# Routing beside RWKV6 with one operand in PSUM, counts sorted by expert, tables of experts built by segments, and the last piece's sends a page sooner

## The chip, the core and the metric

The kernel runs on one core of one Trainium2 chip. The metric is the device time of one execution in microseconds (us); less is better. All data are 32-bit floats.

## What is computed

The input x has 4 sequences of 1024 tokens with 256 channels. Four blocks are added to it, each behind a layer norm:

```python
x = x + retention(layernorm(x))   # 16 heads, decay mask, group norm, gate
x = x + moe(layernorm(x))         # 8 experts, the best 2 of each token
x = x + rwkv6(layernorm(x))       # a recurrence over 1024 tokens, 16 heads of 16x16 states
x = x + moe(layernorm(x))         # the same experts
```

In the MoE the two highest of eight logits of a token choose its experts; their softmax weights, normed to a sum of one, weigh the two results. An expert is `silu(gate) * up` of 256 to 2 x 256 channels, and a product back to 256.

## The kernel before, in words

Retention, MoE, RWKV6 and MoE again follow one another, with some overlap at the borders. A tile has 128 partitions.

**MoE.** Tokens are sorted by expert through DRAM. The 4096 tokens are 32 tiles; they come in three pieces (`Piece`, called m or next_a for the first 16 tiles, mid and end for 8 each). For each piece `logits` makes the router's products on PE, `biased` (L524) adds the bias on DVE, and `routing` (L534 to L730), a generator that `route` advances by one part a call, works on DVE: a token's two best experts (`m_top`, `m_eq`, `m_where`, `m_hot`, `m_rest`, L553 to L563), their softmax (`m_dif`, `m_ex`, `m_den`, `m_tag`, L573 to L584), the tokens before it with the same expert by two matmuls with triangles of ones (`m_rank`, L589 and L590), counts and prefix sums (`m_cnt`, `m_run`, L593 and L595), pages of each expert (`m_more`, `m_pages`, `m_first`), and each token's two rows in the sorted table (`m_off`, `m_eq`, `m_atf`, `m_at`, L675 to L694). The last part makes the table of experts (`m_reach`, `m_of`, `m_ofi`, L702 to L730): which expert's weights each of 71 pages needs. `send` then writes a token tile: ACT makes `m_row` (L495, and L735 for the tags), and POOL issues two indirect DMAs to `xg_all` (L737).

`tiles` then goes over the 71 pages of 128 rows. In iteration j PE transposes page j+1 (`m_xtp`, L781; ACT copies it to `m_xt`, L783), multiplies page j (`m_hp`, L788), transposes page j-1 (`m_atp`, L818) and multiplies page j-2 (`m_op`, L825). ACT makes `m_sg` (L792), DVE `m_a` (L794) and `m_aT` (L820) and, for each group of four pages, `m_share` and `m_to` (L803 to L813). ACT weighs the result (`m_y`, L830), and POOL sends it back (L831, `y_all`). Pages are loaded from `xg_all` in groups of four by SP (L770). Pages 0 to 24 hold tokens of the first piece only, so their work starts while mid and end are still routed and sent; page 25 and later ones wait for all sends. A dictionary names what else comes in which iteration (`add(j, f)`): routing, sends, and the finish of the stage before.

**RWKV6.** Eight blocks of 512 tokens, each of eight steps (step 8j + n) of two halves. In a half DVE multiplies (`w_vb`, L1094) and makes two scans (`w_s`, L1096), POOL multiplies by r (`w_s`, L1104), and PE sums (`w_yp`, L1127). PE, ACT, DVE and POOL prepare the next block beside that (`w_pp`, L1008; `w_dp`, L964; `w_xf`, L974 to L978) and finish the last one (`w_sq`, L1183; `w_rstd`, L1167; `w_cen`, L1181 and L1182). Piece next_a is routed in steps 44 to 46 and sent from step 47 on; mid's routing begins in steps 61 to 63.

**What sets the order.** PE's and ACT's instructions run in the order in which the program writes them, all through; DVE's and POOL's too from the first MoE on, and SP's in RWKV. In retention the scheduler orders DVE. Small results lie in SBUF. PSUM is given out in banks of 128x512; products take the next of a ring of three (`psum`, tag "mm"), which waits for the bank's former readers. A routing's m_rank takes one of those.

The calls that place routing, sends and tables among the pages are these:

```python
for n in range(PARTS - 3):
    add(n // 2, mid.route)
for i in range(mid.nt):
    add(3 + i, mid.send, i)
...
for n in range(PARTS):
    add(9 + n // 2, end.route)
for i in range(end.nt):
    add(13 + i, end.send, i)
```

Of the kernel before, what the change touches and what calls it, by code (L numbers as in the profile page):

```python
# [53 lines left out]
E = 8  # L54
# [54 lines left out]
def hybrid_kernel(  # L109
# [360 lines left out]
    class Piece:  # L470


        def __init__(self, moe, start, blocks, prev=None):
            self.moe, self.start, self.prev = moe, start, prev
            self.nt = blocks * NT
# [59 lines left out]
        def routing(self):  # L535
            sm, logit, nt = self.sm, self.logit, self.nt

# [8 lines left out]

            tops, hots, wheres = [], [], []
            cur = logit  # L550
            for n in range(2):
                top = sm([HT], f"m_top{n}")
                nc.vector.tensor_reduce(top, cur, AX.X, ALU.max)  # L553
                eq = sm([HT, E], f"m_eq{n}")
                nc.vector.tensor_tensor(eq, cur, wide(top), ALU.is_equal)
                nc.vector.tensor_mul(eq, eq, per(key))
                where = sm([HT], f"m_where{n}")
                nc.vector.tensor_reduce(where, eq, AX.X, ALU.max)
                hot = sm([HT, E], f"m_hot{n}")
                nc.vector.tensor_tensor(hot, eq, wide(where), ALU.is_equal)  # L560
                if n == 0:
                    cur = sm([HT, E], "m_rest")
                    nc.vector.scalar_tensor_tensor(cur, hot, NEG, logit, ALU.mult, ALU.add)  # L563
                tops.append(top)
                wheres.append(where)
                hots.append(hot)
                if n == 0:
                    yield
# [3 lines left out]
            dif = sm([HT], "m_dif")  # L572
            nc.vector.tensor_sub(dif, tops[1], tops[0])  # L573
            ex = sm([HT], "m_ex")
            nc.scalar.activation(ex, dif, AF.Exp)
            yield
            den = sm([HT], "m_den")
            nc.vector.tensor_scalar_add(den, ex, 1.0)
            tag = self.tag = sm([HT, 4], "m_tag", bufs=2)
            nc.vector.reciprocal(tag[:, :, 0], den)  # L580
            nc.vector.scalar_tensor_tensor(
                tag[:, :, 1], ex, -1.0, tag[:, :, 0], ALU.add, ALU.mult)
            nc.vector.tensor_copy(tag[:, :, 2], dest[:, self.start * NT : self.start * NT + nt])
            nc.vector.tensor_scalar(  # L584
                tag[:, :, 3], wheres[0], -1.0, float(E), ALU.mult, ALU.add)
            both = both.rearrange("p i e -> p (i e)")

            rp = psum([P, 2, nt * E], "m_rank")
            mm(rp[:, 0, :], lhsT=before, rhs=both, start=True, stop=True)  # L589
            mm(rp[:, 1, :], lhsT=every, rhs=both, start=True, stop=True)  # L590
            yield
            cnt = sm([E, HT], "m_cnt")
            nc.vector.tensor_copy(cnt, rp[:, 1, :].rearrange("p (i e) -> p e i", e=E))  # L593
            run = sm([E, HT], "m_run")
            nc.vector.tensor_tensor_scan(  # L595
                run.rearrange("p e i -> p (e i)"), chains[nt],
                cnt.rearrange("p e i -> p (e i)"), 0.0, ALU.mult, ALU.add,
            )

            def pages(name, total, n, op=ALU.is_gt, first=0):  # L600
                more = (ph if n == HT else px).tile([P, E, n], F32, name="m_more", tag=f"m_more{n}")
                nc.vector.tensor_tensor(
                    more, each(total, n), steps[:, first : first + n].unsqueeze(1).to_broadcast(
                        [P, E, n]), op)
                t = sm([E], name)
                nc.vector.tensor_reduce(t, more, AX.X, ALU.add)
                return t
# [17 lines left out]
            prev, last = self.prev, run[:, :, nt - 1]  # L625
            cap = sm([E], "m_cap")
            self.segments = []
            if prev is None:

                self.total = last  # L630
                full = pages("m_whole", last, HT, ALU.is_ge, 1)
                self.pages = pages("m_pages0", last, HT)
                part = sm([E], "m_part")
                nc.vector.tensor_sub(part, self.pages, full)
                f, behind = firsts("m_first0", full, 0.0)
                self.segments.append(f)
                nc.vector.tensor_scalar_mul(cap, full, float(P))
                low = sm([E], "m_low")
                nc.vector.tensor_scalar_mul(low, f, float(P))
                f, self.used = firsts("m_first1", part, behind)  # L640
                self.segments.append(f)
                self.counts = sm([E], "m_counts0")
                nc.vector.tensor_copy(self.counts, last)
                high = begins("m_high0", f, cap)
                shifted = low
            else:
                k = prev.order + 1
                self.counts = sm([E], f"m_counts{k}")
                nc.vector.tensor_add(self.counts, prev.counts, last)
                self.pages = pages(f"m_pages{k}", self.counts, TT)  # L650
                part = sm([E], "m_part")
# [4 lines left out]
                low = prev.open  # L656
                high = begins(f"m_high{k}", f, cap)
                shifted = sm([E], "m_low")
                nc.vector.tensor_add(shifted, low, prev.counts)
            self.order = 0 if prev is None else prev.order + 1  # L660
            rise = sm([E], "m_rise")
            nc.vector.tensor_sub(rise, high, low)

            if prev is None:
                self.open = high
            else:
                self.open = sm([E], f"m_open{self.order}")
                nc.vector.scalar_tensor_tensor(
                    self.open, part, 0.0, rise, ALU.is_gt, ALU.mult)
                nc.vector.tensor_add(self.open, self.open, low)  # L670
            nc.vector.tensor_add(cap, cap, low)
            yield

            off = sm([E, HT], "m_off")
            nc.vector.tensor_sub(off, run, cnt)  # L675
            nc.vector.tensor_add(off, off, each(shifted))
            slot = sm([HT, E], "m_eq0")
            nc.vector.tensor_add(
                slot, rp[:, 0, :].rearrange("p (i e) -> p i e", e=E),
                off.rearrange("p e i -> p i e"),  # L680
            )
            new = sm([HT, E], "m_eq1")
            nc.vector.tensor_tensor(new, slot, per(cap), ALU.is_ge)
            nc.vector.tensor_mul(new, new, per(rise))
            nc.vector.tensor_add(slot, slot, new)
            yield
            self.at = []
            for n in range(2):
                t = sm([HT, E], "m_rest")
                nc.vector.tensor_mul(t, hots[n], slot)  # L690
                f = sm([HT], f"m_atf{n}")
                nc.vector.tensor_reduce(f, t, AX.X, ALU.add)
                a = sm([HT], f"m_at{n}", I32, bufs=2)
                nc.vector.tensor_copy(a, f)  # L694
                self.at.append(a)
            yield
# [3 lines left out]
            if prev is None:  # L700
                lo, n, parts = 0, FULL, self.segments[:1]
            else:  # L702
                lo, n, parts = FULL, NSL - FULL, self.segments
            if prev is not None and self.start + nt // NT < NBLK:
                return
            at = number[:, lo : lo + n]
            where = ph if lo == 0 else px
            of = where.tile([P, n], F32, name="m_of", tag=f"m_of{lo}")
            for k, f in enumerate(parts):
                reach = where.tile(  # L710
                    [P, n, E - 1], F32, name="m_reach", tag=f"m_reach{lo}")
                nc.vector.tensor_tensor(
                    reach, at.unsqueeze(2).to_broadcast([P, n, E - 1]),
                    f[:, 1:E].unsqueeze(1).to_broadcast([P, n, E - 1]), ALU.is_ge)
                if k == 0:
                    nc.vector.tensor_reduce(of, reach, AX.X, ALU.add)
                    continue
# [5 lines left out]
                if k == 2:  # L723
                    yield
            ofi = where.tile([P, n], I32, name="m_ofi", tag=f"m_ofi{lo}")
            nc.vector.tensor_copy(ofi, of)
            for j in range(n):
                moe.ofi[lo + j] = ofi[0:1, j : j + 1]
            moe.ofs.append((lo, of))
# [707 lines left out]
    PARTS = 8  # L1437
    m, mid = moes[0].pieces[:2]
    for i in range(CHUNKS):
# [12 lines left out]
        if i in (24, 25):  # L1452
            for _ in range(PARTS // 2):
                m.route()
        if i >= 26:
# [7 lines left out]
    for _ in range(3):  # L1463
# [18 lines left out]
    def pieces_sent(mid, end, logits):  # L1482

        for n in range(PARTS - 3):
            add(n // 2, mid.route)
        for i in range(mid.nt):
            add(3 + i, mid.send, i)
# [3 lines left out]
        for n in range(PARTS):  # L1491
            add(9 + n // 2, end.route)
        for i in range(end.nt):
            add(13 + i, end.send, i)
# [17 lines left out]
    add(7, end.block, 1)  # L1512
    pieces_sent(mid, end, ((0, 7), (1, 9)))
# [36 lines left out]
    for n in range(PARTS):  # L1550
        add(44 + n // 3, next_a.route)
    for n in range(3):
        add(61 + n, mid.route)
# [27 lines left out]
    add(6, end.block, 1)  # L1581
    pieces_sent(mid, end, ((1, 8),))
# [124 lines left out]
```

## Time and profile before

| what | value |
|---|---|
| median of 3 runs (lowest, highest) | 1609.24 us (1603.85, 1613.45) |
| profiled execution: its time, its span | 1602.58 us, 1600.8 us |
| mean granted clock of PE | 0.898 |
| busy: PE, DVE, POOL, ACT | 1358.1, 1017.4, 925.8, 604.6 us |
| RWKV6, from the first to the last w_s | about 675 to 1297 us |
| pages 0 to 24 of the first MoE | about 355 to 482 us |
| pages 0 to 24 of the second MoE | about 1299 to 1427 us |

A row of a timeline gives start, duration in us, engine, line, operation, result and operands with their shapes, a count, and in brackets the idle time of the engine before it and what released it. In the chain of waits, a row is a piece of the chain that ended last; "issue" is time in which an engine waited for nothing that the profile shows. PE, DVE, ACT and POOL are TensorE, VectorE, ScalarE and GpSimd; SP issues most DMAs.

### The profile page before, as it was taken

The page shows a single profiled execution, that of the slowest core. Times are in us where ns is not written, and L with a number is a line of the kernel's source. Part 1 is how long each engine was busy: PE and PEld are TensorE (multiplying, and loading weights), DVE is VectorE, ACT ScalarE, POOL GpSimd, SP SyncE. Part 2 cuts the span into 40 slices and gives each one's busy share as a digit, 9 for nine tenths or more (in the row PEclk, how much of TensorE's full clock was granted, in tenths as well). Part 3 has the DMA queues.
Part 4 walks back from the last instruction along what each step waited for, and adds up shares of the span by engine and source line. Part 5 has one row for each costly group of instructions (what it writes and reads, how often), then busy time and mean ns, then how long its engine had stood idle before and what let it go on. Part 6 is the DMA issues. An engine that isn't in the chain of part 4 may idle for free.

```text
span 1600.8 us, 21021 instructions
## 1 busy us (share of the span) xinstructions
PE 1358.1 (85%) x6652; PEld 715.6 (45%) x6652; DVE 1017.4 (64%) x2004; ACT 604.6 (38%) x1436; POOL 925.8 (58%) x881
## 2 busy tenths in 40 slices
PE   5999999878889988987879798887697587889993
PEld 3667666545545544422223233332232234456562
DVE  6566557424433443387988898999989962523444
ACT  2343434433433334443343434442344224333331
POOL 4233322744463326399999898986599844453331
PEclk9999999968899999998989798997789778899997
DMA  8991111231333431266655444533346832232545
GB/s 294 331 321 54 54 45 49 72 119 56 125 102 102 133 111 55 63 150 149 166 140 154 119 133 112 150 105 106 98 126 162 258 110 77 90 108 93 187 130 181
DMA packets 117548, 207.70 MB, mean 130 GB/s; under 512 B 12193, under 2 KB 80001, under 8 KB 117441
## 3 DMA queue, kind: packets, MB, share of 16 engines
q1 hardware_dynamic: 95904, 160.20, 34.7%
q0 software_dynamic: 17184, 39.86, 8.0%
q10 hardware_dynamic: 4352, 6.29, 1.3%
q8 instruction: 57, 0.93, 0.2%
q14 instruction: 51, 0.41, 0.1%
HBM read 139.18 MB, written 67.14 MB: 129 GB/s over the span
## 4 chain that ended last, share of the span: by engine, by line
PE 53%; DVE 18%; POOL 13%; ACT 6%; issue 5%; DMA 4%; SPq 0%; DVEq 0%; POOLq 0%; ACTq 0%
PE m_hp L788 13%; PE m_op L825 6%; DVE w_s L1096 5%; POOL w_s L1104 5%; PE w_pp L1008 4%; PE a_qkp L291 3%; DVE w_vb L1094 2%; PE a_yp L350 2%; PE w_dp L964 2%; PE m_lp L520 2%; PE w_yp L1127 2%; PE a_sp L330 2%; POOL xg_all L737 2%; PE a_gp L273 2%; PE m_xtp L781 2%
## 5 line engine op out<-in xcount | busy, mean ns | idle before, releaser
L1104 POOL TENSOR_TENSOR w_s<-w_s,w_rT 128x1024 f32<-128x1024 f32 x128 | 304.2, 2417 | 33.9 <-DVE w_s L1096 30.3
L831 POOL DMA_INDIRECT y_all<-m_y,m_to x142 | 137.6, 969 | 300.6 <-ACT m_xt L783 171.2
L788 PE MATMUL m_hp<-w1a,m_xt 128*128 x568 | 287.7, 632 | 15.2 <-ACT m_xt L783 11.8
L794 DVE TENSOR_TENSOR m_a<-m_hp,m_sg 128x256 f32<-128x256 f32 x142 | 60.1, 423 | 292.6 <-ACT m_sg L792 292.5
L1094 DVE TENSOR_TENSOR w_vb<-w_vb,w_wk 128x1024 f32<-128x1024 f32 x128 | 153.3, 1198 | 30.5 <-ACT w_wk L1037 26.6
L1096 DVE TENSOR_TENSOR_SCAN w_s<-w_wk,w_carry,w_vb 128x512 f32<-128x512 f32 x128 | 160.9, 1275 | 9.3 <-PE w_yp L1127 1.2
L1096 DVE TENSOR_TENSOR_SCAN w_s<-w_wk,w_vb 128x512 f32<-128x512 f32 x128 | 152.8, 1215 | 13.3 <-ACT w_carry L1114 5.9
L825 PE MATMUL m_op<-w2a,m_aT 128*128 x568 | 152.7, 393 | 6.2 <-DVE m_aT L820 4.5
L737 POOL DMA_INDIRECT xg_all<-m_row,m_at x128 | 125.8, 982 | 43.5 <-issue 29.2
L788 PEld LDWEIGHTS m_hp<-w1a,m_xt 128*128 128x128 f32 x568 | 103.9, 204 | 91.8 <-issue 78.4
L1127 PE MATMUL w_yp<-w_s,core_c 128*32 128x512 f32 x512 | 101.2, 690 | 45.3 <-POOL w_s L1104 34.8
L792 ACT ACTIVATE m_sg<-m_hp 128x256 f32<-128x256 f32 x142 | 54.5, 384 | 165.3 <-PE m_hp L788 165.3
L303 POOL TENSOR_TENSOR a_t<-a_t,a_t 128x512 f32<-128x512 f32 x32 | 41.1, 1285 | 125.9 <-DVE a_t L302 94.1
L830 ACT ACTIVATE m_y<-m_op,m_share 128x256 f32<-128x256 f32 x142 | 67.3, 474 | 119.6 <-PE m_op L825 119.6
L977 POOL TENSOR_TENSOR w_xf<-w_xf,w_sx 128x512 f32<-128x512 f32 x72 | 94.1, 1307 | 24.3 <-ACT w_xf L976 23.6
L825 PEld LDWEIGHTS m_op<-w2a,m_aT 128*128 128x128 f32 x568 | 99.9, 196 | 18.0 <-ACT m_sg L792 3.6
L978 POOL TENSOR_TENSOR w_xf<-w_xf,w_xT 128x512 f32<-128x512 f32 x80 | 87.2, 1093 | 5.6
L333 DVE TENSOR_TENSOR a_pt<-a_sp,ret_c 128x2048 f32<-128x2048 f32 x32 | 73.2, 2286 | 17.6 <-PE a_sp L330 17.5
L818 PEld LDWEIGHTS m_atp<-cst,m_a 128*128 128x128 f32 x284 | 40.6, 146 | 90.3 <-issue 65.9
L781 PE MATMUL m_xtp<-cst,m_xg 128*128 128x128 f32 x284 | 58.6, 290 | 15.2 <-DMA m_xg<-xg_all 15.2
L783 ACT COPY m_xt<-m_xtp 128x256 f32<-128x256 f32 x142 | 51.9, 366 | 42.8 <-PE m_xtp L781 42.6
L291 PE MATMUL a_qkp<-wqkv,a_xT 128*128 128x512 f32 x128 | 65.9, 641 | 0.0
(251 smaller groups left out, 2461.0 us busy)
## 6 DMA issues: line engine op xcount, KB each, us to landing
w_vb<-v_all SPq DMA_DIRECT2D x125, 512.0 KB
xg_all<-zero SPq DMA_DIRECT2D x34, 520.0 KB
m_xg<-xg_all SPq DMA_DIRECT2D x34, 520.0 KB
tab<-in_rope SPq DMA_DIRECT2D x32, 512.0 KB
m_back<-y_all SPq DMA_DIRECT2D x48, 256.0 KB
v_all<-w_vT SPq DMA_DIRECT2D x64, 128.0 KB
res<-in_x SPq DMA_DIRECT2D x8, 512.0 KB
w1a<-in_w SPq DMA_DIRECT2D x8, 512.0 KB
```

Source lines behind the costliest of these rows:

```text
L291: mm(qkp, lhsT=xc[:, c, cols], rhs=wqkv[:, c, 0 : 2 * C], start=(c == 0), stop=(c == KC - 1))
L737: nc.gpsimd.indirect_dma_start(out=self.moe.sends[2 * (self.start * NT + i) + n][:, :], out_offset=bass.IndirectOffsetOnAxis(ap=self.at[n] ...
L781: nc.tensor.transpose(tp[:, c, :], self.xg[g][:, i, c * P : (c + 1) * P], ident)
L788: mm(hp, lhsT=self.xt[j][:, c, :], rhs=w1a[:, bass.ds(self.ev[j], 1), c, :].rearrange("p o n -> p (o n)"), start=(c == 0), stop=(c == KC - 1))
L825: mm(op, lhsT=self.aT[j][:, c, :], rhs=w2a[:, bass.ds(self.ev[j], 1), c, :].rearrange("p o n -> p (o n)"), start=(c == 0), stop=(c == KC - 1))
L831: nc.gpsimd.indirect_dma_start(out=self.scatters[j][:, :], out_offset=bass.IndirectOffsetOnAxis(ap=self.to[g][:, i : i + 1], axis=0), in_= ...
L977: nc.gpsimd.tensor_mul(xf, xf, sx)
L978: nc.gpsimd.tensor_add(xf, xf, d["now"][:, c, :])
L1094: nc.vector.tensor_mul(vb, vb, wk[:, 1:2, :].to_broadcast([P, 2, BLK]))
L1096: nc.vector.tensor_tensor_scan(s[:, q, 1 : BLK + 1], wk[:, 0, :], vb[:, q, :], 0.0 if j % NB == 0 else st[j - 1]["carry"][:, n, 2 * h + q ...
L1104: nc.gpsimd.tensor_mul(s[:, :, 0:BLK], s[:, :, 0:BLK], d["r"][:, g, :].unsqueeze(1).to_broadcast([P, 2, BLK]),)
L1127: mm(d["yp", g][32 * q : 32 * q + 32, :], lhsT=w["sel"][:, i, :], rhs=d["s", n, q // 2][:, q % 2, 0:BLK], start=False, stop=(i == 3), skip ...
```

## The change

- In the piece next_a (`apart`), routing's temporaries lie in two PSUM banks: the choice of experts in a bank m_choice, the later ones in the bank of m_rank. So each two-input DVE operation of it has at most one operand in SBUF. ACT copies hot0 and the counts (128x128 each) to SBUF.
- In all six pieces the two matmuls take m_both sorted by expert, so ranks and counts come out sorted, the copy m_cnt goes, and slots are computed in that order. den, reciprocal and tag follow the scan.
- The table of experts is a method, `table(k)`, for one segment a call. Routing has 6 parts (4 in next_a) in place of 8.
- The calls move. Retention: the first piece is routed in chunks 24 and 25 (three parts each) with its table in 25; mid gets 2 parts there (3 before). First MoE: mid's parts in iterations 1, 1, 2, 3 (0, 0, 1, 1, 2 before). Second MoE: 1, 2, 3 (the same five before). Both: mid's sends in iterations 4 to 11 (3 to 10), end's parts in 9, 9, 10, 11, 11, 11 (two each in 9 to 12), end's sends in 12 to 19 (13 to 20), tables in 6, 7, 14 and 18 (all with end's last part in 12). RWKV6: next_a's parts in steps 44, 44, 45, 46 (three, three and two in 44 to 46), its table in step 62 (46).

The diff, cut to its core:

```diff
+            self.apart = prev is None and moe.layer == 1
...
+        def bank(self, name):
+            self.room = psum([P, 512], name)
+            self.col = 0
+
+        def tmp(self, shape, name):
+            if not self.apart:
+                return self.sm(shape, name)
+            n = int(np.prod(shape))
+            t = self.room[:, self.col : self.col + n]
+            self.col += n
+            return t if len(shape) == 1 else t.rearrange("p (a b) -> p a b", b=shape[1])
...
+            if self.apart:
+                self.bank("m_choice")
...
+            eq = tmp([HT, E], "m_eq")
             for n in range(2):
-                top = sm([HT], f"m_top{n}")
+                top = (tmp, sm)[n]([HT], f"m_top{n}")
...
-                hot = sm([HT, E], f"m_hot{n}")
+                hot = (tmp, sm)[n]([HT, E], f"m_hot{n}")
...
             nc.scalar.activation(ex, dif, AF.Exp)
+            if self.apart:
+                hot = sm([HT, E], "m_hot0")
+                nc.scalar.copy(hot, hots[0])
+                hots[0] = hot
             yield
...
-            both = both.rearrange("p i e -> p (i e)")
-            rp = psum([P, 2, nt * E], "m_rank")
+            both = both.rearrange("p i e -> p e i")
+            rp = psum([P, 512], "m_rank")
+            self.room, self.col = rp, 2 * nt * E
...
-            cnt = sm([E, HT], "m_cnt")
-            nc.vector.tensor_copy(cnt, rp[:, 1, :].rearrange("p (i e) -> p e i", e=E))
-            run = sm([E, HT], "m_run")
+            if self.apart:
+                each_cnt = sm([E, HT], "m_cnt")
+                nc.scalar.copy(each_cnt, cnt)
+            else:
+                each_cnt = cnt
+            run = tmp([E, HT], "m_run")
...
+        def table(self, k):
...
-        for n in range(PARTS - 3):
-            add(n // 2, mid.route)
         for i in range(mid.nt):
-            add(3 + i, mid.send, i)
+            add(4 + i, mid.send, i)
...
         for n in range(PARTS):
-            add(9 + n // 2, end.route)
+            add((9, 9, 10, 11, 11, 11)[n], end.route)
         for i in range(end.nt):
-            add(13 + i, end.send, i)
+            add(12 + i, end.send, i)
+        add(6, mid.table, 0)
+        add(7, mid.table, 1)
+        add(14, mid.table, 2)
+        add(18, end.table, 3)
...
+    for n, j in enumerate((1, 1, 2, 3)):
+        add(j, mid.route)
...
-    for n in range(PARTS):
-        add(44 + n // 3, next_a.route)
-    for n in range(3):
-        add(61 + n, mid.route)
+    for n in (44, 44, 45, 46):
+        add(n, next_a.route)
+    add(62, next_a.table, 0)
+    for n in (61, 62, 63):
+        add(n, mid.route)
...
+    for n, j in enumerate((1, 2, 3)):
+        add(j, mid.route)
```

## The prediction

> **What bounds the kernel now.** I read the table of 40 slices first (no engine fills the span), then the page's chain:
>
> ```profile
> PE 53%; DVE 18%; POOL 13%; ACT 6%; issue 5%; DMA 4%; SPq 0%; DVEq 0%; POOLq 0%; ACTq 0%
> ```
>
> The bound changes by stage, so I took timelines where the change edits. First the DVE, then POOL, in RWKV's steps 44 to 47:
>
> ```profile
> 1094.28 1.46 DVE L555 TENSOR_TENSOR m_eq<-m_logit,m_top 128x128 f32<-128x128 f32 x1
> 1095.77 1.24 DVE L556 TENSOR_TENSOR m_eq<-m_eq,cst 128x128 f32<-128x128 f32 x1
> 1097.05 0.29 DVE L558 TENSOR_REDUCE m_where<-m_eq 128x16 f32<-128x128 f32 x1
> 1097.37 1.99 DVE L560 TENSOR_TENSOR m_hot<-m_eq,m_where 128x128 f32<-128x128 f32 x1
> ...
> 1116.06 2.56 DVE L595 TENSOR_TENSOR_SCAN m_run<-cst,m_cnt 128x128 f32<-128x128 f32 x1
> ...
> 1123.03 0.29 DVE L685 TENSOR_TENSOR m_eq<-m_eq,m_eq 128x128 f32<-128x128 f32 x1
> ...
> 1325.92 0.30 DVE L1164 SCALAR_TENSOR_TENSOR w_varp<-w_varp,q_y 128x128 f32<-128x128 f32 x1
> ```
>
> ```profile
> 1096.83 2.38 POOL L1104 TENSOR_TENSOR w_s<-w_s,w_rT 128x1024 f32<-128x1024 f32 x1
> ...
> 1128.76 2.35 POOL L1104 TENSOR_TENSOR w_s<-w_s,w_rT 128x1024 f32<-128x1024 f32 x1 [10.43 <-DVE w_s L1096]
> ```
>
> A 128x128 operation with two SBUF inputs takes 0.29 us when POOL is idle (L685) and up to 1.99 beside it; m_hot ends at 1099.36, where POOL's w_s ends (1099.21). The reduce with one input, 0.29, isn't held. POOL then idles 10.43 us for the DVE: routing is on the path there.
>
> In the first MoE, PE, then POOL:
>
> ```profile
> 367.84 2.63 PE L788 MATMUL m_hp<-w1a,m_xt 128*128 x4 [3.14 <-DVE m_eq L678]
> ...
> 376.59 3.78 PE L788 MATMUL m_hp<-w1a,m_xt 128*128 x4 [3.80 <-ACT m_xt L783]
> ...
> 445.02 0.69 PE L818 MATMUL m_atp<-cst,m_a 128*128 128x128 f32 x2 [3.61 <-DVE m_a L794]
> 446.59 2.04 PE L825 MATMUL m_op<-w2a,m_aT 128*128 x4 [0.88 <-DVE m_aT L820]
> ...
> 481.94 0.66 PE L781 MATMUL m_xtp<-cst,m_xg 128*128 128x128 f32 x2 [4.92 <-DMA m_xg<-xg_all]
> ```
>
> ```profile
> 442.80 1.16 POOL L737 DMA_INDIRECT xg_all<-m_row,m_at  x1 [0.30 <-DVE m_ofs L721]
> 449.42 0.96 POOL L831 DMA_INDIRECT y_all<-m_y,m_to  x1 [5.46 <-ACT m_y L830]
> ...
> 475.19 0.96 POOL L737 DMA_INDIRECT xg_all<-m_row,m_at  x1 [0.30 <-issue]
> ```
>
> DVE's 6.4 us of tables (438.15 to 444.64) stop PE, which starves POOL for 5.46 us; from there POOL issues back to back, and page 25's load waits for its last send. The second MoE repeats this (PE waits 3.60, 0.87 and 4.92 us); the chain shows the end:
>
> ```profile
> 1420.20 2.46 DMA xg_all<-m_row,m_at
> 1422.84 4.00 DMA m_xg<-xg_all
> 1426.97 0.53 PE m_xtp L781 x2
> ```
>
> **RWKV (next_a's routing).** Step 44: from 1093.99 to 1105.68, seven held operations cost 1.46 + 1.24 + 1.99 + 1.24 + 0.81 + 1.23 + 0.81 = 8.78 us; at 0.29 each (2.03) they save 6.7. Gone too is the wait for m_ex (0.28). den, reciprocal and tag (0.6) move to step 46: nothing. m_run goes from 2.56 to about 0.42 (an unheld 128x128 scan in retention): 2.1. The copy m_cnt: 0.27. The table (0.31 + 0.34 + 1.92 = 2.57, step 46) moves to step 62. Sum 11.9; added: the first PSUM write waits for ACT's reading of that bank's former tile, 0.7 by the ACT row near 1094.7. Queued behind it on DVE are step 45's scans, which POOL waits for. Net 11.2.
>
> [...] But L1164 on PSUM takes 0.30, L685 on SBUF 0.29, and only strided reads more (L678 0.37). [...] Copies of hot0 and counts go to ACT, 38% busy, at an estimated 0.2 to 0.4 each (m_xt's copy of 256 is 0.37); the routing's second half comes two steps (7 us) later and hides them; uncovered, 0.7.
>
> Does POOL take over? Its queue ends at 1104.08, then only w_s of 2.36 a scan pair, and its 10.43 us idle is larger than what is taken out. And PE: m_choice and m_rank hold two of the ring of three banks, the latter to the last routing operation; w_pp (L1008) now waits for that. Before, it had 12 us of lead. Its chain runs about 7 us, its product is needed some 10.6 us after step 47 starts: estimated slack 3.7; for w_dp 3. Cost 0 to 3, taken 0. At step 62 the table pays again: 0.6 for its two first operations, 0.2 to 1.9 for the cast, of which some falls into a POOL operation the next routing row would wait out anyway: 1.2. RWKV: -10 (range -5 to -11.5). Sends and weight loads follow the steps in program order.
>
> **First MoE, opening.** The retention tail's a_mean to a_shift now stand ahead of mid's scan on DVE. a_shift came at 371.85 behind 4.7 us of routing; it becomes a_var (366.5) + POOL's a_rs 1.3 + three operations = 368.4, 3.5 sooner. ACT's a_yn and m_xt follow, so hp at 376.59 does too. The 3.14 stop vanishes but this second wait absorbs it. The scan's 3.5 us then lie in ACT's time. Net -3.5 (0 to -5).
>
> **Each MoE, pages 9 to 25.** Now: burst idle 3.61 + 0.88, the first row of routing 0.60, slow matmuls after it (m_op 2.04 instead of 1.03, m_hp 2.91 for 1.88, two transposes +0.55) 2.6: 7.7 us. After: end's second half is one 6.35 us block at iteration 11. From the steady rows, m_a waits 2.27 for ACT and is needed 2 us later still, so DVE has 4.27 us a page: stop 2.1, and slow matmuls about 1 (after 1.14 idle they lost 0.07, after 3.14 some 1.6). The tables come in four parts of 1.05 to 1.9 us (L712 to L726: 0.49 + 0.49 + 0.26 + 0.25 + 0.21, the last with a cast of 0.19), under 4.27: 0 each, 1 at worst. PE: -4.6. POOL: the block ends near 439.5 and the first end pair is out by 441.8; y resumes at 442.3, not 449.42, and 7 x 3.8 us (three issues of 1.27) bring the last send to 467.7 instead of 475.2. Mid's sends, one page later (ACT 0.77, two issues), fill POOL's idle before 430 (8.35). Load: 467.7 + 2.4 + 3.9 + 0.3 = 474.4, PE 481.94 before: -7.5, both MoEs alike (range -2 to -9); the shorter idle may give 0.9 more. The second MoE's opening hangs on the finish of RWKV (PE waits 4.70 for w_rstd, POOL's w_sq 3.81), which routing doesn't move: 0 (-1 to +1). Counts by expert elsewhere: six copies of 0.2 hidden in retention and pages, 0.
>
> **Sum.** -10 - 3.5 - 7.5 - 7.5 = -28.5 from 1602.6 (span 1600.8, 1.8 around it): 1574. That execution lay 6.7 below the median of the runs, 1609.2, against which I set it: 1581.
>
> **Rivals.** *Only RWKV comes through* (0.2): the block at iteration 11 stops PE like the old one (4.5 + 2.6) and the pages end where they did. For it: the same length. Against: the old block met a DVE already 1.5 us late. -10: 1599. *The PSUM form is still held by POOL, or the waiting banks give it back* (0.13): RWKV 0, pages as above: -18.5: 1591. Against: L1164, w_vb L1094 hold their pace beside POOL. *DVE becomes the bound in the pages* (0.07, the slower side): there is no 4.27 us of cover; each block costs 7.1, each of eight tables its 1.7 and 1 for slow matmuls after it: 2 x 7.1 + 8 x 2.7 = 35.8, against 2 x 7.7 paid now: +20.4, with RWKV -10: 1620, and no opening gain. It decides when a table costs PE over 1.4 us (2 x 7.1 + 8 x 1.4 = 15.4 + 10); it speaks against this that the routing's 3.3 us at 1375.3 cost PE only 1.14.
>
> **Numbers.** Likeliest, 0.6: 1581, own range 1571 to 1592. A measurement tells 0.5% (8 us) from no change. Range 1570 to 1601 takes in the first two rivals. Faster 0.86, same 0.06, slower 0.08.
>
> **What would show it.** Step 44's rows at 0.3 us beside POOL; step 47 starting 11 us sooner after step 44; POOL's 5.46 idle gone and PE's 4.92 at page 25 near 2; a stop of about 2 us at iteration 11. Wrong if PSUM rows are held, if w_pp or w_dp ends DVE's waits at steps 47 to 49, or if tables stop PE.

## The result, and the profile after

| kernel | median (lowest, highest), runs | profiled execution: time, span, granted clock of PE |
|---|---|---|
| before | 1609.65 us (1603.85, 1617.35), 8 | 1602.58, 1600.8, 0.898 |
| after | 1594.61 us (1582.56, 1597.83), 8 | 1597.25, 1595.5, 0.897 |

The ratio is 0.9887, with an interval from 0.9863 to 0.9911: 15.0 us or 1.1% faster. The forecast was 28 us (1581), so a little over half of it came: 1594.6 lies in the stated range, 1570 to 1601, but outside the likeliest one, 1571 to 1592. The shares of the chain of waits after:

```profile
PE 58%; DVE 16%; POOL 12%; ACT 6%; issue 4%; DMA 3%; another core or an unknown queue 1%; SPq 0%; DVEq 0%; POOLq 0%; ACTq 0%
```

DVE lost two points of the chain and PE gained five. The new item, "another core or an unknown queue", stands for waits whose releaser the profile could not name; they come up again below.

**RWKV, steps 44 to 47.** DVE's timeline after, where the rows of 1.46, 1.24 and 1.99 stood before, then POOL's and PE's:

```profile
1097.81 0.29 DVE L570 TENSOR_REDUCE m_choice<-m_logit 128x16 f32<-128x128 f32 x1 [0.72 <-ACT w_xf L986]
1098.14 0.29 DVE L571 TENSOR_TENSOR m_choice<-m_logit,m_choice 128x128 f32<-128x128 f32 x1
...
1099.12 0.30 DVE L576 TENSOR_TENSOR m_choice<-m_choice,m_where 128x128 f32<-128x128 f32 x1
```

```profile
1098.55 1.27 POOL L1193 TENSOR_TENSOR w_sq<-w_cen,w_gT 128x512 f32<-128x512 f32 x1
1099.77 2.34 POOL L1114 TENSOR_TENSOR w_s<-w_s,w_rT 128x1024 f32<-128x1024 f32 x1
```

```profile
1127.34 6.53 PE L1018 MATMUL w_pp<-w_xf,w_r 128*128 128x512 f32 x8 [5.63 <-DVE m_at L709]
```

Each of the 128x128 operations with an operand in PSUM takes 0.29 or 0.30 us in step 44, beside POOL operations that read SBUF. The bank's former reader costs 0.72, at the first write only. PE does wait 5.63 us for the second bank, and nobody waits for PE: from step 47 to the second half of step 62 (w_vb at 1127.20 and 1271.03) RWKV takes 143.8 us in both kernels.

**RWKV, steps 62 and 63.** DVE's timeline after, then POOL's:

```profile
1274.73 2.54 DVE L723 TENSOR_TENSOR m_reach<-cst,m_first 128x175 f32<-128x175 f32 x1
...
1279.04 5.22 DVE L586 TENSOR_TENSOR m_both<-m_hot,m_hot 128x64 f32<-128x64 f32 x1
```

```profile
1279.53 4.65 POOL L1114 TENSOR_TENSOR w_s<-w_s,w_rT 128x1024 f32<-128x1024 f32 x2
1288.88 2.34 POOL L1114 TENSOR_TENSOR w_s<-w_s,w_rT 128x1024 f32<-128x1024 f32 x1 [4.70 <-DVE w_s L1106]
```

The table pushes mid's routing back by 3 us. The wait that m_eq had before (2.19 us, now 0.23) falls to the table's first row. But routing's last operation of that shape, m_both, 0.23 us in its old place, now meets two POOL operations that follow each other without a gap, and is held until both are done. DVE's scans come late, and POOL idles 4.70 us for them. The sum comes out: 3.06 us for the table's three rows, less 1.96 for m_eq, and 4.99 more for m_both make the 6.1 of the table below.

**Pages of the first MoE.** PE's timeline after, then ACT's:

```profile
443.94 0.44 PE L828 MATMUL m_atp<-cst,m_a 128*128 128x128 f32 x2 [1.73 <-DVE m_a L804]
...
462.07 1.98 PE L798 MATMUL m_hp<-w1a,m_xt 128*128 x4 [2.09 <-issue]
466.01 0.44 PE L828 MATMUL m_atp<-cst,m_a 128*128 128x128 f32 x2 [1.95 <-DVE m_a L804]
```

```profile
447.40 0.47 ACT L840 ACTIVATE m_y<-m_op,m_share 128x256 f32<-128x256 f32 x1 [2.46 <-remote]
...
458.11 0.47 ACT L840 ACTIVATE m_y<-m_op,m_share 128x256 f32<-128x256 f32 x1 [3.26 <-issue]
...
461.65 0.37 ACT L793 COPY m_xt<-m_xtp 128x256 f32<-128x256 f32 x1 [2.50 <-remote]
```

The old stop for DVE's tables (3.61 us) has shrunk to 1.73, and page 25's wait for its load (4.92) is gone. But ACT now starts late by 2.5 to 3.3 us, three times in 15 us, and the profile names no engine that it waits for ("remote" is a releaser that it does not know). I call these late starts. PE's rows come late with them, and pages 15 to 23 take 4.3 us each where the trace before had 3.02.

**Stage by stage.** Two conditions must be matched before traces are subtracted. First, chunks 16 to 24 of retention take 85.5 us in some traces and 89 to 93 in others, of one and the same kernel; the granted clock goes with it in all fourteen traces of this case: 85.5 us at a mean of 0.98 (four traces), 89.3 to 90.3 at 0.92 or 0.93 (three), 92.8 to 93.2 at 0.89 or 0.90 (seven). Two traces of the kernel before show it (the second is e4 below; the clock is the column after POOL's, 0.83 or 1.00). The one shown with the prediction, then e4:

```profile
165.00:185.00 20.00, 19.63 (x122) 12.96 (x119) 12.13 (x21) 8.20 (x21) 2.61 (x2) 0.83 0.18 52
...
225.00:245.00 20.00, 19.80 (x157) 14.09 (x150) 7.20 (x16) 6.18 (x15) 4.03 (x7) 0.83 0.09 27
```

```profile
165.00:185.00 20.00, 19.64 (x191) 13.73 (x190) 12.90 (x27) 10.30 (x24) 4.36 (x5) 1.00 0.21 63
...
225.00:245.00 20.00, 18.82 (x191) 12.77 (x191) 11.07 (x19) 7.52 (x21) 4.84 (x7) 1.00 0.18 53
```

That is 7.4 us which no edit made. Second, the late starts: e4's trace of the kernel before has them too, the first one has none. So the column "after less e4" compares like with like; times in us.

| stage (from, to) | before, first trace | before, e4 | after | after less e4 |
|---|---|---|---|---|
| retention's end (a_pt of chunk 24, first m_a) | 102.64 | 108.95 | 109.04 | +0.1 |
| MoE 1 opening (m_a of pages 0 and 9) | 54.38 | 52.75 | 49.16 | -3.6 |
| MoE 1, pages 9 to 15 | 36.24 | 35.12 | 31.67 | -3.4 |
| MoE 1, pages 15 to 23 | 24.17 | 30.87 | 34.50 | +3.6 |
| MoE 1, pages 23 to 25 | 12.68 | 8.29 | 6.04 | -2.2 |
| RWKV, middle of step 44 to step 47 (w_vb) | 45.14 | 45.12 | 34.59 | -10.5 |
| RWKV, middle of step 62 to middle of 63 (w_vb) | 11.54 | 11.53 | 17.62 | +6.1 |
| from there to page 9 of MoE 2 | 76.54 | 76.74 | 73.93 | -2.8 |
| MoE 2, pages 9 to 16 | 33.58 | 33.56 | 27.82 | -5.7 |
| MoE 2, pages 16 to 23 | 21.15 | 27.51 | 32.99 | +5.5 |
| MoE 2, pages 23 to 25 | 12.85 | 6.72 | 6.04 | -0.7 |

Before rounding, the last column sums to -13.8; the stages not listed add -3.4 outside retention. One pair of traces settles a stage to a few us only: with e0's trace of the change in place of the first, the column sums to -16.3 and the stages not listed add +1.8.

### The profile page after: what moved, and what is told of

Same layout as the page of the kernel before. It is cut to its first block, busy times and chain, and to the rows that moved or that the text cites. A ratio compares the mean times of both kernels' runs of the same rounds, so it can differ in the third digit from the quotient of the medians.

```text
span 1595.5 us, 21015 instructions
## 1 busy us (share of the span) xinstructions
PE 1363.2 (85%) x6652; PEld 719.3 (45%) x6652; DVE 1013.1 (63%) x1998; ACT 603.1 (38%) x1438; POOL 925.1 (58%) x881
## 4 chain that ended last, share of the span: by engine, by line
PE 58%; DVE 16%; POOL 12%; ACT 6%; issue 4%; DMA 3%; another core or an unknown queue 1%; SPq 0%; DVEq 0%; POOLq 0%; ACTq 0%
PE m_hp L798 14%; PE m_op L835 7%; DVE w_s L1106 5%; POOL w_s L1114 4%; PE w_pp L1018 4%; PE a_qkp L291 3%; DVE w_vb L1104 2%; PE a_yp L350 2%; PE w_yp L1137 2%; PE w_dp L974 2%; POOL w_xf L987 2%; PE m_lp L521 2%; PE a_sp L330 2%; PE m_atp L828 2%; PE m_xtp L791 2%
## 5 line engine op out<-in xcount | busy, mean ns | idle before, releaser
L1137 PE MATMUL w_yp<-w_s,core_c 128*32 128x512 f32 x512 | 105.5, 718 | 45.8 <-POOL w_s L1114 35.6
L291 PE MATMUL a_qkp<-wqkv,a_xT 128*128 128x512 f32 x128 | 67.6, 655 | 0.0
L1137 PEld LDWEIGHTS w_yp<-w_s,core_c 128*32 128x32 f32 x512 | 16.5, 118 | 110.2 <-POOL w_s L1114 59.5
```

Source lines behind the costliest of these rows:

```text
L291: mm(qkp, lhsT=xc[:, c, cols], rhs=wqkv[:, c, 0 : 2 * C], start=(c == 0), stop=(c == KC - 1))
L1137: mm(d["yp", g][32 * q : 32 * q + 32, :], lhsT=w["sel"][:, i, :], rhs=d["s", n, q // 2][:, q % 2, 0:BLK], start=False, stop=(i == 3), skip ...
```

## The experiments

Each ratio is against runs of the kernel before on the same chip. The change itself gives 0.9887; 0.001 is 1.6 us.

**e0: the change once more, unedited.**

> The changed kernel once more, unedited, for a second trace of it. In the first trace ACT, DVE and PE start several instructions late in the two MoEs' sends (m_y, m_xt and m_sg near 458 to 465 us, about 7 us, m_sg near 1399, 4 us, a_yT near 354, 5.6 us) with no releaser that the trace shows. Theory: these are chance, or come from the run; then the second trace has none or has them elsewhere, its span is some 10 us shorter than 1595 or as long with the loss in other places. Rival: they belong to the change (sends that follow one another without a gap); then the same instructions of pages 14 to 18 are late again by 4 to 8 us. Time: about 0.989 of the kernel before by both.

1594.84 us, ratio 0.9886 (0.9844 to 0.9928). It repeats. So do the late starts, partly in other instructions: the last a_yT waits 9.70 us, as in the first trace (9.59), and m_sg in the pages 2.52 and 3.82. Pages 9 to 25 take 72.21 us in the first MoE, as before, and 64.40 in the second, where the first trace has 66.85.

**e1: next_a's table back in step 46.**

```diff
-    add(62, next_a.table, 0)
+    add(46, next_a.table, 0)
```

> The changed kernel with next_a's table of experts back in step 46, behind the last routing part, where POOL is idle. Theory: in step 62 the table's 3.1 us push mid's m_both into two of POOL's w_s (5.22 us instead of 0.23), and the move costs 6 us there; in step 46 it costs 0.31 + 0.34 + 0.18 = 0.8. So 5 us less than the changed kernel (ratio to the kernel before about 0.986 if the changed one is at 0.989). Rival: POOL's chain in steps 62 and 63 sets the end of RWKV either way, and m_both's wait is slack: no difference, or 0.8 us more.

1589.56 us, ratio 0.9846 (0.9808 to 0.9884). Steps 62 to 63 fall from 17.62 to 11.60 us, and the table costs 0.83 in step 46. m_both is back at 0.22; m_eq takes the one wait instead, as before the change, in DVE's timeline of e1:

```profile
1272.45 2.20 DVE L571 TENSOR_TENSOR m_eq<-m_rest,m_top 128x64 f32<-128x64 f32 x1
...
1275.52 0.22 DVE L586 TENSOR_TENSOR m_both<-m_hot,m_hot 128x64 f32<-128x64 f32 x1
```

The place of the stop is shown. Its worth in the total is less sure: e8 and e9 also have the table in step 46, and the three average 0.9862, against 0.9883 for the three with it in step 62 (after, e0, e5): 3.4 us. Part of the stop is regained before page 9 of MoE 2 (73.93 us, 76.18 in e1).

**e2: no operand in PSUM.** Everything else of the change stays; next_a's six parts spread over the same steps.

```diff
-            self.apart = prev is None and moe.layer == 1
+            self.apart = False
...
-    for n in (44, 44, 45, 46):
+    for n in (44, 44, 45, 46, 46, 46):
```

> The changed kernel with next_a's routing temporaries in SBUF (no PSUM banks, no copies by ACT), its parts in steps 44, 44, 45 and three in 46. Theory of the held operand: seven 128x128 operations take 8.8 us instead of 2.0 beside POOL, the scan up to 2.6 instead of 0.4, so 7 to 9 us more than the changed kernel; m_rank's bank is needed the same way. Rival, PSUM as such gives nothing (POOL's queue or the held bank takes it back): within 2 us of the changed kernel.

1601.35 us, ratio 0.9919 (0.9896 to 0.9942), 5 to 7 us given back, a little less than expected; the two intervals just overlap (0.9896 against 0.9911). The stage is clearer: the stretch from step 44 to 47 takes 41.88 us in place of 34.59. DVE's timeline of e2 has the held rows again:

```profile
1096.74 1.44 DVE L571 TENSOR_TENSOR m_eq<-m_logit,m_top 128x128 f32<-128x128 f32 x1
1098.21 1.24 DVE L572 TENSOR_TENSOR m_eq<-m_eq,cst 128x128 f32<-128x128 f32 x1
```

Further on, an operation with a single input is held too, beside one POOL operation (DVE's row, then POOL's):

```profile
1124.96 2.31 DVE L621 TENSOR_SCALAR m_den<-m_ex 128x16 f32<-128x16 f32 x1
```

```profile
1124.90 2.34 POOL L1114 TENSOR_TENSOR w_s<-w_s,w_rT 128x1024 f32<-128x1024 f32 x1 [1.34 <-DVE w_s L1106]
```

In the change, which writes it to PSUM, it takes 0.18 us beside the same POOL operation. So 7.3 of the 10.5 us belong to the operand in PSUM.

**e3: the pages' calls as before.** Mid's sends in 3 to 10, end's parts two each in 9 and 11 and one each in 10 and 12, end's sends in 13 to 20, all four tables in iteration 12.

```diff
-            add(4 + i, mid.send, i)
+            add(3 + i, mid.send, i)
...
-            add((9, 9, 10, 11, 11, 11)[n], end.route)
+            add((9, 9, 10, 11, 11, 12)[n], end.route)
...
-            add(12 + i, end.send, i)
+            add(13 + i, end.send, i)
...
-        add(6, mid.table, 0)
-        add(7, mid.table, 1)
-        add(14, mid.table, 2)
-        add(18, end.table, 3)
+        for k in range(4):
+            add(12, (mid, mid, mid, end)[k].table, k)
```

> The changed kernel with the page placement of before: mid's sends in iterations 3 to 10, end's parts in 9, 9, 10, 11, 11, 12, end's sends in 13 to 20, all four tables in 12. Theory of the prediction: the tables' 6.4 us stop PE for 4.5 us and 2.6 us of slow matmuls, and the last send is 7 us later, in each MoE: 10 to 15 us more than the changed kernel. Rival by the two traces (page 25 came only 0.8 to 1 us sooner than the page-5 shift explains): 2 us more in both MoEs together.

1601.53 us, ratio 0.9941 (0.992 to 0.9962), 7 to 9 us slower than the change, between the two expectations. Pages 9 to 25 take 77.87 us in place of 72.21, and 70.48 in place of 66.85 in MoE 2.

**e4: the kernel before, unedited.**

> The kernel before once more, unedited, for a second trace. Its first trace (1602.6 us) has none of the late starts of ACT that both traces of the changed kernel have at the same places (a_yT at the end of retention 5.6 us late, m_y and m_sg of pages 14 to 18, some 7 us in the first MoE and 4 to 6 in the second), though the instructions and waits around a_yT are the same in both kernels. Theory: they belong to an execution's conditions, not to the change, and the first trace of before was a lucky one; then this trace shows them, its span is 5 to 12 us above 1600.8, and page by page the changed kernel is shorter than this one by what was predicted. Rival: the change makes them; then this trace has none, as the first.

1606.75 us, ratio 0.9991 (0.9964 to 1.0018). Late starts are there: the last a_yT of retention waits 9.59 us ("remote"; 3.99 in the first trace), an m_y in the pages 4.74. They come with the execution, not with the change, so this is the trace to subtract from.

**e5: only the sends of end a page later, as before.**

```diff
-            add(12 + i, end.send, i)
+            add(13 + i, end.send, i)
```

> The changed kernel with end's sends in iterations 13 to 20 again, all else as changed. Theory of the prediction: POOL's last send is one page (3.0 to 3.8 us) later in each MoE and page 25 waits for it: 4 to 7 us more than the changed kernel. Rival: with the tables spread, POOL catches up its page before the last send: within 2 us of the changed kernel.

1593.02 us, ratio 0.9877 (0.9841 to 0.9913): no loss seen. Pages 9 to 25 take 71.36 us. In these traces the sends' page is worth nothing.

**e6: only the tables together, in iteration 12.**

```diff
-        add(6, mid.table, 0)
-        add(7, mid.table, 1)
-        add(14, mid.table, 2)
-        add(18, end.table, 3)
+        for k in range(4):
+            add(12, (mid, mid, mid, end)[k].table, k)
```

> The changed kernel with all four tables in iteration 12, behind the routing block of 11. Theory: 6.4 us of DVE behind a 6.35 us block, with 4.27 us of cover a page: PE stops about 4 us more per MoE and loses 2 to 3 to slow matmuls, and POOL's sends wait for m_y: 5 to 12 us more than the changed kernel in both together. Rival: page 25 waits for POOL's last send anyway, and what PE loses is hidden in that wait: within 3 us.

1600.3 us, ratio 0.9926 (0.9897 to 0.9955), about 6 us slower, though the two intervals overlap. The stage is clear: pages 9 to 15 take 38.55 us in place of 31.67. PE's timeline of e6 has the stop of before:

```profile
452.28 0.69 PE L828 MATMUL m_atp<-cst,m_a 128*128 128x128 f32 x2 [4.20 <-DVE m_a L804]
453.85 2.05 PE L835 MATMUL m_op<-w2a,m_aT 128*128 x4 [0.88 <-DVE m_aT L830]
```

With e5 this says that of the pages' edits the spread of the tables is what pays.

**e7: what is left** without the operand in PSUM, with the table in step 46 and the pages' calls of e3: counts by expert, fewer parts, and the new opening.

> Only the rest of the change: next_a's routing in SBUF with its table in step 46, the page placement of before (end's parts, end's and mid's sends, tables in 12), but the counts by expert, the six-part routing and mid's parts in iterations 1, 1, 2, 3. Theory: left is the first MoE's opening (a_shift ahead of the scan, 3.5 us): 2 to 5 us less than the kernel before. Rival, no part of it matters: within 1.5 us.

1602.48 us, ratio 0.9951 (0.9928 to 0.9975): 7.5 us faster than before, more than expected. The trace shows 4.0 in the opening (48.73 us) and 2.4 from step 44 to 47 (42.74 us).

**e8: more buffers for what POOL's indirect DMAs read,** with e1's table.

```diff
-            row = ph.tile([P, W], F32, name="m_row", tag="m_row", bufs=6)
+            row = ph.tile([P, W], F32, name="m_row", tag="m_row", bufs=7)
...
-            y = px.tile([P, C], F32, name="m_y", tag="m_y", bufs=4)
+            y = px.tile([P, C], F32, name="m_y", tag="m_y", bufs=8)
```

> The changed kernel with next_a's table back in step 46, and more buffers for what POOL's indirect DMAs read: m_y 8 for 4, m_row 7 for 6. To be set against the changed kernel with the table in step 46 alone (1589.6 us, 0.985 of before). Theory, rings: ACT's late starts in pages 17 to 23 (m_y at 447.40 and 458.11 of the changed kernel's trace, up to 3.3 us each) are waits for a buffer whose scatter has not landed; with 8 there is none, pages 9 to 25 take about 67.5 us instead of 71.2 in each MoE, and the time falls by 3 to 8 us, to 1582 to 1587. Rival, not the rings: m_xt and m_sg, which read no such buffer, start late too, so the late starts stay, pages 9 to 25 stay within 1 us, and the time stays at 1588 to 1592.

1587.76 us, ratio 0.9859 (0.9821 to 0.9896), as e1. Pages 15 to 23 take 35.00 us, and late starts of up to 4.6 us remain in the pages. So m_y's buffers are not the cause; m_row got only one more, which says less.

**e9: e1 and e5 together.**

> The changed kernel with the table in step 46 and end's sends in iterations 13 to 20 as before the change. Theory: the two edits are independent; the table's place is worth 5 to 6 us, the sends' page nothing: 1587 to 1591, 0.983 to 0.987 of before, pages 9 to 25 at 71 to 72 us. Rival: with the sends a page later the load of page 25 comes last again, +2 to +4 a MoE: 1593 to 1598.

1592.73 us, ratio 0.988 (0.9842 to 0.9918). The median lies between the two expectations; pages 9 to 25 take 71.55 us, as the theory has it, though page 25 waits for its load again (PE 1.09 us).

**e10: results of pages 12 to 19 scattered twice,** to the same rows.

```diff
-            nc.gpsimd.indirect_dma_start(
-                out=self.scatters[j][:, :],
-                out_offset=bass.IndirectOffsetOnAxis(ap=self.to[g][:, i : i + 1], axis=0),
-                in_=y, in_offset=None,
-            )
+            for _ in range(2 if 12 <= j < 20 else 1):
+                nc.gpsimd.indirect_dma_start(
+                    out=self.scatters[j][:, :],
+                    out_offset=bass.IndirectOffsetOnAxis(ap=self.to[g][:, i : i + 1], axis=0),
+                    in_=y, in_offset=None,
+                )
```

> The changed kernel with one cost doubled: in both MoEs the results of pages 12 to 19 are scattered twice to the same rows, so POOL issues one more indirect DMA of 1.27 us in each of eight iterations beside end's sends. Theory, POOL's issues bound the pages: 8 x 1.27 = 10.2 us less the 6 us that POOL idles there in the changed kernel's trace, +4 to +10 a MoE, time +8 to +20: 1603 to 1615. Rival, POOL has slack and PE's stalls come from ACT: POOL's idle takes it up, at most +1.5 a MoE: 1594 to 1598.

1620.95 us, ratio 1.0032 (1.0004 to 1.0061), 23 us slower than the change: POOL has no slack, more so than expected, since the second scatter also waits for the first to land (2.27 us in the row at 451.16). Of more interest are the first pages of the stretch, before the backlog reaches ACT. POOL's timeline of e10, then DVE's of m_a there:

```profile
446.67 0.96 POOL L747 DMA_INDIRECT xg_all<-m_row,m_at  x1 [0.30 <-issue]
447.93 0.96 POOL L842 DMA_INDIRECT y_all<-m_y,m_to  x1 [0.30 <-ACT m_sg L802]
451.16 0.96 POOL L842 DMA_INDIRECT y_all<-m_y,m_to  x1 [2.27 <-DMA y_all<-m_y,m_to]
```

```profile
450.89 0.42 DVE L804 TENSOR_TENSOR m_a<-m_hp,m_sg 128x256 f32<-128x256 f32 x1 [2.26 <-ACT m_sg L802]
...
453.92 0.42 DVE L804 TENSOR_TENSOR m_a<-m_hp,m_sg 128x256 f32<-128x256 f32 x1 [2.27 <-issue]
...
456.94 0.42 DVE L804 TENSOR_TENSOR m_a<-m_hp,m_sg 128x256 f32<-128x256 f32 x1 [0.98 <-ACT m_sg L802]
```

Here POOL pauses about 2 us after each fourth issue, and five pages go by in 3.02 us each: no late starts, in a trace that has one of 9.74 in retention and one of 8.24 after these pages, where the backlog reaches ACT (m_y waits 4.69 and 5.42 us for y_all's DMA at 467.64 and 474.07). In the change's trace, twelve issues without a pause (448.15 to 463.02) go with the late starts at 458.11 and 461.65. But a long row of issues is not enough: the first trace of the kernel before has twenty (454.90 to 479.94) without a late start.

**e11: pauses made by spreading the sends,** with e1's table.

```diff
-            add(12 + i, end.send, i)
+            add((12, 13, 15, 17, 19, 21, 22, 23)[i], end.send, i)
```

> The changed kernel with the table in step 46 and end's eight sends spread over iterations 12, 13, 15, 17, 19, 21, 22 and 23, so that POOL pauses between them. With the scatter doubled, where POOL waited 1.7 to 2.7 us after every fourth issue, ACT's late starts in pages 14 to 19 were gone (3.02 us a page in place of 4.7). Theory, late starts come of long rows of indirect DMAs that POOL issues without a pause: pages 15 to 22 take 3.0 to 3.2 us each, page 25 then waits 4 to 7 us for its load, pages 9 to 25 take 64 to 69 us in each MoE (71 to 72 with the sends of the change), time 1579 to 1588. Rival, late starts come with POOL's issues whatever their spacing: pages 15 to 22 stay at 4 us or more, the wait for the load comes on top, pages 9 to 25 take 73 to 78 us, time 1593 to 1602.

1583.59 us, but the kernel before took only 1600.04 on this chip: ratio 0.9925 (0.989 to 0.9959), no better than the change. Pages 15 to 23 take 24.17 us (3.02 each), then PE waits in e11's timeline for the last send:

```profile
469.11 0.66 PE L791 MATMUL m_xtp<-cst,m_xg 128*128 128x128 f32 x2 [11.43 <-DMA m_xg<-xg_all]
```

Pages 9 to 25 take 74.61 us, more than the theory had. It doesn't decide on the pauses: this trace has no late start anywhere, in retention neither, where nothing was spread (last a_yT 3.98). It gives something else, the first half of the pages after the change (sends spread, table in step 46) without late starts, to set against the first trace of before: pages 9 to 15 in 30.68 us in place of 36.24, and 9 to 16 of MoE 2 in 25.96 in place of 33.58.

## Why the prediction was right, and by half in size

- **RWKV, steps 44 to 47: right.** 11.2 forecast, 10.5 measured. The rows stand at the predicted 0.3, the bank's reader at 0.72 (0.7). No routing operation of next_a with an operand in PSUM is held (128x128 at most 0.30 us, the scan 0.40), but two with one input, from SBUF to SBUF, are: m_den (2.31 in e2) and the cast m_ofi (1.92 in the kernel before). The prediction has that cast in its 2.57, but did not take it for a held operation. An operand in PSUM costs no time of its own here: 0.29 to 0.30, where operations on SBUF alone take 0.29 with POOL idle.
- **Held banks: right,** PE waits 5.63 us and its slack covers it. POOL does not take over.
- **Table in step 62: the term 1.2 was too small.** It priced the table's rows against the POOL operation that the next routing row would wait out anyway, and that part came (3.06 less 1.96 is 1.1). It left out where the table pushes the later rows: m_both waits 5.22 us behind two POOL operations. Measured +6.1, of which about 2 are regained at MoE 2's opening. And the move saved only 0.83 us in step 46 (e1), not the 2.57 forecast: the cast is not held there any more.
- **MoE 1 opening: right.** 3.5 forecast, 3.6 to 4 measured. PE's second wait, for m_xt, remains (4.68 us at 382.29). **MoE 2 opening:** 0 forecast; the regained part lies there.
- **Each MoE's pages, -7.5: wrong in one step.** Its PE half is right: -4.6 forecast for the stop and the slow matmuls; -5.6 and -7.6 without late starts (e11 against the first trace), -3.4 and -5.7 with them; e6 shows that it is the tables' spread. The step that failed is the last of its sum, the load of page 25. It took that load to end last, before and after, with PE and ACT at 3.02 us a page, as in the trace I had. In e4's trace of the kernel before, pages 23 to 25 take only 2.2 and 0.7 us over the 6.04 that they take without a wait, so no more could be won there. The last send does leave sooner, 56.5 us after page 9 (62.1 in e4), though POOL stops twice for m_y in the change:

```profile
448.15 0.95 POOL L841 DMA_INDIRECT y_all<-m_y,m_to  x1 [2.26 <-ACT m_y L840]
...
466.13 0.95 POOL L841 DMA_INDIRECT y_all<-m_y,m_to  x1 [3.12 <-ACT m_y L840]
...
476.72 0.96 POOL L747 DMA_INDIRECT xg_all<-m_row,m_at  x1 [0.30 <-issue]
```

But then PE, held up in pages 15 to 23 (4.3 us a page), ends last and not the load, so the sends' page, which I counted on, is worth nothing (e5). Measured net: -2.1 and -0.9 in the table's pair of traces. More traces say more: in the seven with late starts and the tables spread (after, e0, e1, e2, e5, e8, e9) pages 9 to 25 take 71.5 and 65.5 us on average (70.8 to 72.2 and 64.3 to 67.6), in the three with the old page calls (e3, e4, e7) 75.4 and 68.7 (74.2 to 77.9 and 67.8 to 70.5). That is -3.9 and -3.2, in keeping with e3's 7 to 9 us: half of what was forecast. No trace of the change itself is without late starts, so what the pages would gain there is not measured.
- **Sum.** -28.5 forecast. In the table's pair, the pages' 2 x 7.5 came as 3.0 (+12.0), step 62 as +6.1 for +1.2 (+4.9), MoE 2's opening as -2.8, the RWKV gain 0.7 smaller and the opening 0.1 larger: -13.8. With the pages at 7.1 it would be -17.9. The medians say -15.0, between the two.
- **The rivals.** None came: steps 44 to 47 are not held, DVE doesn't bound the pages, and the pages' PE stop did shrink. The range held because it reached to rivals that gave the pages or RWKV less, for other reasons; to that extent it held by luck.

**Open:** what makes the late starts. m_y's buffers do not (e8), and the change does not (e4). Two traces of fourteen have none: the first one of before, and e11. The trace also records each semaphore event, and there ACT is seen to wait for PE. In 45 of 51 late starts of over 1.9 us (the last a_yT, and the pages to 25 in both MoEs) it starts within 0.1 us of an event of PE's semaphore, and that event comes 1.5 to 5.5 us after PE's row ends, where 0.014 us is the median. Whether PE is really late is not shown, for in the same twelve traces records are missing: 29 to 37% of the events that tell that one of POOL's indirect DMAs has landed, against 0.3 to 0.4% in the other two, and 34 to 51 of PE's 1343 or 1344 events, against none. So the delay may belong to the recording. No run separates the two.

The best versions are those with the table in step 46 (e1 0.9846, e8 0.9859); their intervals overlap that of the change.

## What to carry to other kernels

An operand in PSUM freed each DVE operation here from the POOL operation beside it at no price in its own duration (0.29 to 0.30 us), but two-input operations that stay in SBUF, and one-input ones from SBUF to SBUF such as m_den (held 2.31 us) and the cast m_ofi (1.92), must be placed against POOL's queue: 3 us of table ahead of m_both set it in front of two POOL operations (5.22 us in place of 0.23). Before a saving is credited to a stage with several engines near their pace, take a second trace of the same kernel: what was steady in one (3.02 us a page, a load that ends last) may be neither in the next.

## What the hardware showed unasked

- The granted clock of PE in retention was 0.83 in one execution and 1.00 in another of the same kernel, for stretches of 20 us and more, worth 7.4 us.
- In twelve traces of fourteen ACT stood idle up to 9.8 us (4.0 at the same place in the other two); retention's last part takes 109 to 111 us with it and 102.2 to 102.6 without. PE's semaphore event came 5.3 to 5.5 us after PE's row there, in each of the twelve.
- One DVE operation of 0.23 us was held for 5.22 us, over two POOL operations in a row (4.65), not only over the one that it met.
- A DVE operation with a single input, 128x16 from SBUF to SBUF, was held 2.31 us by one POOL operation of 2.34; with its result in PSUM it took 0.18 beside the same operation.
